# Moving loads, stores and a norm's root within the schedule of a state-space and spectral kernel

## The chip, the cores and the metric

The kernel runs on one core of a Trainium2 chip. The metric is the device time of one execution in microseconds; a kernel's time is the median of several runs. A profile of one execution gives the time of every instruction on the five engines: PE (TensorE, matmuls; PEld is its weight loads), DVE (VectorE), ACT (ScalarE), POOL (GpSimd) and SP (SyncE, which here only issues DMAs).

## The reference

Two layers run one after the other on x of shape (4, 128, 128, 128): batch, channel, height, width. Layer 0 is a selective state-space scan along the 16384 pixels of an image, and a group norm:

```python
h1 = relu(xf @ mlp_w1.T + mlp_b1)
xm = h1 @ mlp_w2.T + mlp_b2
x_in, z = split(xm @ in_proj_w.T, 2)
u = silu(causal_conv4(x_in) + conv_b)
dt, Bm, Cm = split(u @ x_proj_w.T, [8, 24])
delta = softplus(dt @ dt_proj_w.T + dt_proj_b)
A = -exp(A_log)                                  # 256 x 16
def step(h, (d_t, B_t, C_t, u_t)):               # h: batch x 256 x 16
    h = h * exp(d_t[:, :, None] * A) + d_t[:, :, None] * B_t[:, None, :] * u_t[:, :, None]
    return h, einsum('bds,bs->bd', h, C_t)
y = (scan(step) + u * D) * silu(z)
out = y @ out_proj_w.T
x1 = silu(group_norm(out, 4 groups) * gn_w + gn_b) + x
```

Layer 1 filters x1 in the Fourier plane. Weights over four filters come from the image itself:

```python
a = relu(einsum(agg_w, group_norm(concat[x1, x1], 32 groups)) + agg_b)
weights = softmax(mean(a) @ wg_w.T + wg_b)       # batch x 4
xf = rfft2(x1)
ff = rfft2(irfft2(xf[:, None] * wc))             # wc: 4 complex filters a channel
out = irfft2(sum_f weights_f * xf * ff_f) + residual_weight * x1
```

## The kernel before

**Block 0.** An image is cut into 32 chunks of 512 pixels, and the four images make 128 chunks, k = 0 to 127. A chunk takes 16 slots of one hand-written order; slot n of the program belongs to chunk n // 16. In each slot DVE scans a pair of state rows (`scans`, L389, the scan itself in L405), for which ACT has made the decay factors `da` one slot ahead (`exps`, L387) and POOL the inputs `hb` two slots ahead (`dbu`, L354), from copies of delta, du, B and C over the partitions. PE turns one of the inputs by a transpose into PSUM (`b`, L374) and sums the states (`y`, L426).

The chunk's own preparation (`pre`, L175) is a list of steps. Each has a slot, counted from 16 slots before the chunk's scan begins (so its slot 16 is slot 0 of the chunk), a phase and a function. The slots of all chunks go into one table `todo`. In each slot the phases are taken in the order turn, sums, pe, exps, late, act, pool, dbu, gate, scans, dve, end; an engine executes what it gets in this order. DMAs are nearly all issued by SP, also in this order, and SP waits in place when a DMA's buffer or data is not ready. The steps of the preparation that matter here:

- `load` (slot −9): the chunk's input `xt`, 256 KB, one buffer. Chunk 0's is issued by ACT.
- `h1_mm` (−7), `h1_act` (−6), `xm_mm`, `xm_act` (−5, −4): the two layers on PE and ACT; then `cv_mm`, `silu_act` (0 to 2), `xd_mm`, `xd_act` (3, 4). `xd_act` stores `bc` (rows of B and C) to DRAM.
- `bc_load` (5): eight DMAs, which copy B and C to `rB` and `rC` over the partitions (4 x 192 KB and 4 x 256 KB).
- `dt_act` (6): delta, and its two stores to `dd` in DRAM. `du_pool` (7): du = delta * u on POOL, and its two stores.
- `rep_load(0)` (9) and `rep_load(1)` (16): each four DMAs `rdelta` and four `rdu` from `dd`, 256 KB each.

Seen over the repeating 16 slots, the `load` of chunk k at −9 stands in slot 7 of chunk k − 2, beside the `du_pool` of chunk k − 1, and its `h1_mm` in slot 9.

The first slot of all issues the first constants (`first_constants`, L79). Slot 4 issues the later ones (`later_constants`, L105), slot 8 makes products of them on DVE and PE (`later_products`, L123).

**The norm of an image** (`finish`, L552, with `group_norm`, L501, used twice) is spread over the chunks of the next image; for the fourth image it lies in block 1. `group_norm` starts at slot `at`: sums on DVE and a matmul for the mean over groups, ACT's steps one slot later, and in slot `at + 3` all of `var_mm` (PE, into a PSUM bank), `root_act` (ACT, square root, needs another activation table than the exponential) and `invert` (DVE's reciprocal, after which ACT makes scale and bias, or the weights `weff`). `bias_mm` and `bias_act` of the second norm follow in slot `c + 4`, where `c` is its start. `at` is slot 7 of a chunk for the first norm and slot 8 for the second.

**Block 1** has 64 units (8 channels of one image), each in three slots t of 3, 3 and 2 channels: DFT over the height (`over_h`, PE L791, ACT copies `sa` L793, DVE makes the other half L798), over the width (`over_w`), products with the mixed filter on DVE, and back. ACT multiplies four filter tiles by the weights (`term`, L764), POOL adds them (`mix`, L770). Pools open with block 1, so its first loads wait until block 0 has ended: seven constants (L690 to L701), then the unit's input, then the filters. Filter tiles are loaded four units ahead (L741 to L746), the first two both at unit 0. In slot t = 0 the four terms of unit 0 are made ahead of `over_h(0)`.

Of the kernel before, what the change touches and what calls it, by code (L numbers as in the profile page):

```python
# [26 lines left out]
F32 = mybir.dt.float32  # L27
# [7 lines left out]
T = 512  # L35
# [10 lines left out]
def kernel(ctx: ExitStack, tc: tile.TileContext, a: dict, out: bass.AP):  # L46
    nc = tc.nc
# [57 lines left out]
    def later_constants(s):  # L105
        s.wo = const("wo", [P, NH, C], a["out_wT"].rearrange("(j p) c -> p j c", p=P))
        s.gnw = col("gn_w")
        s.gnb = col("gn_b")
        s.g0 = const("g0", [P, P], a["c_g0"])
        s.g1 = const("g1", [P, P], a["c_g1"])  # L110
        s.gam = col("gn_gamma")
        s.bet = col("gn_beta")
        s.wagg = const("wagg", [P, 2, C], a["agg_wT"].rearrange("(j p) o -> p j o", p=P))
        s.bagg = col("agg_b")
        s.wwg = const("wwg", [P, NF], a["wg_wT"])
        s.bwg = const("bwg", [P, NF], a["wg_b"].partition_broadcast(P))
        s.resw = const("resw", [P, 1], a["residual_weight"].partition_broadcast(P))
        s.eps = cpool.tile([P, 1], F32, tag="eps", name="eps")
        nc.vector.memset(s.eps, EPS)
        s.ones = cpool.tile([P, P], F32, tag="ones", name="ones")  # L120
        nc.vector.memset(s.ones, 1.0)
# [25 lines left out]
def block0(tc, s):  # L147
# [4 lines left out]
    with ExitStack() as ctx:  # L152
# [22 lines left out]
        def pre(k):  # L175
# [64 lines left out]
                    )  # L240

            def xd_act():
                xd = d["xd"] = p2.tile([NX, T], F32, tag="xd", name=f"xd_{k}")
                nc.scalar.copy(xd, ps["xd"][0:NX, :])
                bc = d["bc"] = dbc.tile([2, NS, T], F32, tag="bc", name=f"bc_{k}")
                nc.sync.dma_start(out=bc.rearrange("q s t -> (q s) t"), in_=xd[R:NX, :])
# [59 lines left out]
            def rep_load(j):  # L306
# [4 lines left out]
                        nc.sync.dma_start(out=t[m * DG : (m + 1) * DG], in_=rows)  # L311

            return [
                (-9, "pe", load), (-7, "pe", h1_mm), (-6, "act", h1_act), (-5, "pe", xm_mm), (-4, "act", xm_act),
                (0, "pe", partial(cv_mm, 0)), (1, "pe", partial(cv_mm, 1)), (2, "act", silu_act),
                (NP - 3, "pe", z_mm), (NP - 1, "act", z_act), (NP + 2, "act", z_silu), (3, "pe", xd_mm), (4, "act", xd_act), (5, "pe", dt_mm), (5, "pe", xd_turn),
                (5, "act", bc_load), (6, "act", dt_act), (7, "act", xd_turn_act), (7, "pool", partial(du_pool, 0)),
                (7, "pool", partial(du_pool, 1)), (8, "pe", partial(du_turn, 0)), (9, "act", partial(rep_load, 0)),
                (8, "pool", partial(bt_act, 0, 0, 1)), (9, "act", partial(bt_act, 0, 1, 5)),
                (10, "act", partial(bt_act, 0, 5, 8)), (11, "pe", partial(du_turn, 1)),  # L320
# [180 lines left out]
def group_norm(s, io, b, mat, which, stat, at, then):  # L501
# [40 lines left out]
    def invert():  # L542
# [2 lines left out]

    return [
        (at, "dve", aggregate), (at, "end", mean_mm), (at + 1, "act", spread_act), (at + 3, "pe", var_mm),
        (at + 3, "act", root_act), (at + 3, "dve", invert),
    ]


def finish(s, io, b, first, norm, agg, add="dve"):  # L552
# [96 lines left out]
        ]  # L649
    c = at[2] + 5  # L650
    todo += group_norm(s, io, b, "g1", 1, lambda: g["stat"], c, middle)
    todo += [(c + 4, "pe", bias_mm), (c + 4, "act", bias_act)]
    for i in range(NCH):
        at = agg(i)
        todo += [
# [10 lines left out]
def block1(tc, s):  # L666
# [10 lines left out]
    with ExitStack() as ctx:  # L677
        def pool(name, bufs, **kw):
            return ctx.enter_context(tc.tile_pool(name=name, bufs=bufs, **kw))

        p1 = pool("fc", 1)
        p2 = pool("f2", 2)
        psa = pool("psa", 1, space=PSUM)
        psx = pool("psx", 2, space=PSUM)
# [2 lines left out]
        pso = pool("pso", 1, space=PSUM)  # L687
        psf = pool("psf", 1, space=PSUM)

        def const(name, shape):  # L690
            t = p1.tile(shape, F32, tag=name, name=name)
            nc.sync.dma_start(out=t, in_=s.a[name])
            return t

        fh = const("c_fh", [H, 2 * WF])
        fwr = const("c_fwr", [W, 2 * WF])
        fwi = const("c_fwi", [W, 2 * WF])
        ihc = const("c_ihc", [H, H])
        ihs = const("c_ihs", [H, H])
        iw = const("c_iw", [W, W])  # L700
        sign = const("c_sign", [W, 2 * HH]).rearrange("w (o r k) -> w o r k", o=1, r=2)  # L701


        small = pool("small", 1)
# [35 lines left out]
            u[n].ft = ft  # L740
        loads = defaultdict(list)  # L741
        for k, ft in enumerate(spans):
            at = ft.first - 4
            if k >= KEEP:
                at = max(at, spans[k - KEEP].last)
            loads[max(at, 0)].append(ft)  # L746

        def load_filter(ft):
            ft.t = p2.tile([H, NF, CC, 2 * WF], F32, tag="ft", name=f"ft_{ft.first}", bufs=KEEP)
# [9 lines left out]
        def term(n, f):  # L759

            if 0 <= n < N:
                tag, bufs = ("term", 3) if f else ("wb", 2)
                t = p2.tile([H, CC, 2 * WF], F32, tag=tag, name=f"{tag}_{n}_{f}", bufs=bufs)
                nc.scalar.activation(t, u[n].ft.t[:, f], AF.Copy, scale=s.wts[units[n][1]][0:H, f : f + 1])  # L764
                u[n].terms = [t] if f == 0 else u[n].terms + [t]
# [102 lines left out]
        with tc.manual_schedule():  # L868
            load(0)
            for t in range(3 * N + LAG + 3):  # L870
                n, i = divmod(t, 3)
                if i == 0:
                    for ft in loads[n]:
                        load_filter(ft)
                    load(n + 1)
                    if n == 0:
                        for f in range(NF):
                            term(0, f)
                            if f:
# [107 lines left out]
```

## Time and profile before

| | us |
|---|---|
| median of 3 runs (7317.51 to 7325.34) | 7318.06 |
| profiled execution | 7313.21 |
| its span, first to last instruction | 7311.3 |
| block 0 ends, last ACT step before block 1 (L641) | 6495.6 |

| engine | busy us | share of the span | instructions |
|---|---|---|---|
| PE | 5969.1 | 82% | 25908 |
| DVE | 6949.5 | 95% | 8040 |
| ACT | 6148.7 | 84% | 13583 |
| POOL | 6895.5 | 94% | 3188 |

A chunk of block 0 takes about 50 us. The shares are means over two blocks: in block 0 DVE and POOL are nearly full, in block 1 PE is (192.5 of the 200 us from 7000 to 7200). A wait in the profile is the idle time of an engine ahead of an instruction, put down to what came last; a wait of an engine that has time to spare costs nothing. The DMA engines moved 1246.34 MB, 170 GB/s over the span.

### The profile page before, as it was taken

The page shows a single profiled execution, that of the slowest core. Times are in us where ns is not written, and L with a number is a line of the kernel's source. Part 1 is how long each engine was busy: PE and PEld are TensorE (multiplying, and loading weights), DVE is VectorE, ACT ScalarE, POOL GpSimd, SP SyncE. Part 2 cuts the span into 40 slices and gives each one's busy share as a digit, 9 for nine tenths or more (in the row PEclk, how much of TensorE's full clock was granted, in tenths as well). Part 3 has the DMA queues.
Part 4 walks back from the last instruction along what each step waited for, and adds up shares of the span by engine and source line. Part 5 has one row for each costly group of instructions (what it writes and reads, how often), then busy time and mean ns, then how long its engine had stood idle before and what let it go on. Part 6 is the DMA issues. An engine that isn't in the chain of part 4 may idle for free.

```text
span 7311.3 us, 90639 instructions
## 1 busy us (share of the span) xinstructions
PE 5969.1 (82%) x25908; PEld 2667.5 (36%) x25908; DVE 6949.5 (95%) x8040; ACT 6148.7 (84%) x13583; POOL 6895.5 (94%) x3188
## 2 busy tenths in 40 slices
PE   7788877888778788887777888887877888868999
PEld 2233322233223233232222323332322333348999
DVE  7999999999999999999999999999999999978677
ACT  6888888888888888888888888888888888867876
POOL 6999999999999999999999999999999999977787
PEclk8888888888888889989888898888888888889999
DMA  6666666666777767767777766677777766758666
GB/s 140 162 157 146 160 157 150 157 157 163 191 180 180 183 159 168 170 163 180 181 177 192 169 166 169 163 167 179 177 188 177 178 167 157 174 144 250 186 165 170
DMA packets 864136, 1246.34 MB, mean 170 GB/s; under 512 B 78856, under 2 KB 318608, under 8 KB 863632
## 3 DMA queue, kind: packets, MB, share of 16 engines
q1 hardware_dynamic: 863488, 1240.28, 69.0%
q8 instruction: 204, 3.34, 0.2%
q14 instruction: 300, 2.46, 0.1%
q10 hardware_dynamic: 144, 0.26, 0.0%
HBM read 996.97 MB, written 243.27 MB: 170 GB/s over the span
## 4 chain that ended last, share of the span: by engine, by line
DMA 16%; ACT 16%; DVE 12%; PE 12%; issue 5%; POOL 2%; SPq 1%; DVEq 0%; ACTq 0%; POOLq 0%
ACT da L387 6%; DVE da L405 6%; DMA xt<-in_x 3%; DMA rdelta<-dd 3%; DVE h L405 3%; DMA dd<-delta 2%; DVE hb L407 2%; DMA rB<-bc 2%; DMA of<-ob 2%; PE pp_h L190 2%; ACT L387 1%; DMA xr<-in_x 1%; ACT bt L295 1%; PE y L426 1%; PE pa L791 1%
## 5 line engine op out<-in xcount | busy, mean ns | idle before, releaser
L354 POOL TENSOR_TENSOR hb<-rdu,rB 128x1536 f32<-128x1536 f32 (+2 forms) x1536 | 3605.1, 2364 | 33.3 <-DMA rdu<-dd 28.9
L387 ACT ACTIVATE da<-rdelta,amat 128x512 f32<-128x512 f32 x4096 | 2671.9, 694 | 48.2 <-DVE h L405 45.0
L412 POOL TENSOR_TENSOR hb<-h,rC 128x1024 f32<-128x1024 f32 (+1 forms) x1072 | 2434.8, 2273 | 156.0 <-DVE h L405 140.2
L405 DVE TENSOR_TENSOR_SCAN da<-da,st,hb 128x512 f32<-128x512 f32 x1976 | 2420.8, 1268 | 10.0 <-POOL hb L354 6.7
L426 PE MATMUL y<-hb,sel 128*32 128x512 f32 x8192 | 1331.8, 726 | 4.8 <-POOL hb L412 2.9
L405 DVE TENSOR_TENSOR_SCAN h<-da,st,b 128x512 f32<-128x512 f32 x992 | 1261.4, 1272 | 57.8 <-ACT da L387 40.2
L407 DVE TENSOR_TENSOR hb<-da,rC 128x512 f32<-128x512 f32 x2040 | 1297.1, 675 | 3.0
L405 DVE TENSOR_TENSOR_SCAN h<-da,st,hb 128x512 f32<-128x512 f32 x1000 | 1254.1, 1257 | 6.7 <-ACT da L387 6.4
L374 PE MATMUL b<-ident,bt 128*128 128x128 f32 x4096 | 766.1, 311 | 511.8 <-DVE h L405 395.8
L225 PE MATMUL pp_cv<-xm,wck 128*128 128x512 f32 x2048 | 1027.3, 647 | 24.1 <-ACT zs L219 23.2
L295 ACT ACTIVATE bt<-pt_dut,xdt 128x256 f32<-128x256 f32 x2048 | 836.8, 471 | 139.8 <-PE pt_dut L284 139.6
L374 PEld LDWEIGHTS b<-ident,bt 128*128 128x128 f32 x4096 | 557.0, 159 | 1085.7 <-DVE h L405 683.1
L408 ACT COPY st<-da 128x1 f32<-128x1 f32 x2040 | 282.2, 161 | 657.4 <-DVE hb L407 654.6
L225 PEld LDWEIGHTS pp_cv<-xm,wck 128*128 128x128 f32 x2048 | 403.5, 208 | 708.8 <-issue 473.1
L190 PE MATMUL pp_h<-xt,w 128*128 128x512 f32 x512 | 399.5, 925 | 273.0 <-DMA xt<-in_x 257.9
L770 POOL TENSOR_TENSOR wb<-wb,term 128x1040 f32<-128x1040 f32 x192 | 461.0, 2401 | 91.6 <-ACT term L764 76.1
L284 PE MATMUL pt_dut<-ident,du 128*128 128x128 f32 x1024 | 209.6, 328 | 269.6 <-ACT st L408 260.3
L258 PE MATMUL pp_dt<-xd,wdt 8*128 8x512 f32 x512 | 290.1, 649 | 80.1 <-ACT pp_o L450 79.2
L422 PE MATMUL y<-u,diag 128*128 128x512 f32 x512 | 297.2, 665 | 66.6 <-DVE zs L436 65.2
L303 POOL TENSOR_TENSOR du<-delta,u 128x512 f32<-128x512 f32 x256 | 319.3, 1269 | 25.3 <-ACT delta L266 25.3
L387 ACT ACT_TABLE_LOAD x262 | 336.1, 1283 | 4.6
L284 PEld LDWEIGHTS pt_dut<-ident,du 128*128 128x128 f32 x1024 | 128.8, 158 | 565.5 <-POOL du L303 426.8
(145 smaller groups left out, 8008.9 us busy)
## 6 DMA issues: line engine op xcount, KB each, us to landing
rdelta<-dd SPq DMA_DIRECT2D x1024, 256.0 KB, 4.7
rdu<-dd SPq DMA_DIRECT2D x1024, 256.0 KB, 7.7
rC<-bc SPq DMA_DIRECT2D x512, 256.0 KB, 7.4
rB<-bc SPq DMA_DIRECT2D x512, 192.0 KB, 4.7
dd<-delta SPq DMA_DIRECT2D x256, 256.0 KB, 7.5
dd<-du SPq DMA_DIRECT2D x256, 256.0 KB, 6.5
ft<-in_filt_w SPq DMA_DIRECT2D x104, 520.0 KB, 7.0
ob<-o SPq DMA_DIRECT2D x128, 256.0 KB, 2.1
```

Source lines behind the costliest of these rows:

```text
L190: nc.tensor.matmul(ps["h", j], s.w1[:, j * P : (j + 1) * P], d["xt"], start=True, stop=True)
L225: nc.tensor.matmul(ps["cv", j], w, d["xm"][:, t : t + T], start=t == 0, stop=t == KC - 1)
L284: nc.tensor.transpose(ps["dut"][:, 2 * t + j, :], d["du"][:, j, at : at + P], s.ident)
L295: nc.scalar.activation(d["bt"][:, 2 * h + t, :, q, :], src, AF.Copy, scale=d["xdt"][:, 2 * h + t, R + q : R + q + 1])
L354: nc.gpsimd.tensor_tensor(hb[:, p : p + n, :], d["du", j][:, m : m + n, :], d["B"][:, p - 1 : p - 1 + n, :], ALU.mult)
L374: nc.tensor.transpose(b[:, t * P : (t + 1) * P], src, s.ident)
L387: nc.scalar.activation(d["da", p][q], d["delta", j][:, m, :], AF.Exp, scale=s.amat[:, c : c + 1])
L405: nc.vector.tensor_tensor_scan(o, das[q], b, init, ALU.mult, ALU.add)
L407: nc.vector.tensor_tensor(hb[:, p + q, :], das[q], d["C"][:, p + q, :], ALU.mult)
L412: nc.gpsimd.tensor_tensor(hb[:, ps, :], h[:, q, :], d["C"][:, ps, :], ALU.mult)
L426: nc.tensor.matmul(y[m * DG : (m + 1) * DG, :], s.sel, d["hb", j, r][:, p, :], start=False, stop=r == NG - 1)
L770: nc.gpsimd.tensor_tensor(wb, wb, u[n].terms[f], ALU.add)
```

## The change

Five edits, none of which adds or drops an instruction on a computing engine:

1. `load` is placed at slot −14 instead of −9, ahead of the chunk's `bc` store, and `xd` comes from the pool with one buffer instead of two.
2. For chunk 0 alone, `bc_load` is placed at slot 7 instead of 5: behind delta's stores, in phase order still ahead of du's.
3. The seven constants of block 1 are loaded with the later constants of block 0, into the pool that lives through both blocks.
4. In `group_norm`, root and reciprocal are two and three slots later, and with them `bias_mm` and `bias_act` of the second norm, by three and four slots.
5. In block 1 the terms of unit 0 come after `over_h(0)`, and the second filter tile is loaded at unit 1 instead of 0, after the second unit's input.

```diff
@@ later_constants
         s.resw = const("resw", [P, 1], a["residual_weight"].partition_broadcast(P))
+
+        s.fh = const("c_fh", [H, 2 * WF], a["c_fh"])
+        s.fwr = const("c_fwr", [W, 2 * WF], a["c_fwr"])
+        s.fwi = const("c_fwi", [W, 2 * WF], a["c_fwi"])
+        s.ihc = const("c_ihc", [H, H], a["c_ihc"])
+        s.ihs = const("c_ihs", [H, H], a["c_ihs"])
+        s.iw = const("c_iw", [W, W], a["c_iw"])
+        s.sign = const("c_sign", [W, H], a["c_sign"])
@@ xd_act
-                xd = d["xd"] = p2.tile([NX, T], F32, tag="xd", name=f"xd_{k}")
+                xd = d["xd"] = p1.tile([NX, T], F32, tag="xd", name=f"xd_{k}")
@@ pre
-                (-9, "pe", load), (-7, "pe", h1_mm), (-6, "act", h1_act), (-5, "pe", xm_mm), (-4, "act", xm_act),
+                (-14, "pe", load), (-7, "pe", h1_mm), (-6, "act", h1_act), (-5, "pe", xm_mm), (-4, "act", xm_act),
...
-                (5, "act", bc_load), (6, "act", dt_act), (7, "act", xd_turn_act), (7, "pool", partial(du_pool, 0)),
+                (5 if k else 7, "act", bc_load), (6, "act", dt_act), (7, "act", xd_turn_act), (7, "pool", partial(du_pool, 0)),
@@ group_norm
         (at, "dve", aggregate), (at, "end", mean_mm), (at + 1, "act", spread_act), (at + 3, "pe", var_mm),
-        (at + 3, "act", root_act), (at + 3, "dve", invert),
+        (at + 5, "act", root_act), (at + 6, "dve", invert),
@@ finish
-    todo += [(c + 4, "pe", bias_mm), (c + 4, "act", bias_act)]
+    todo += [(c + 7, "pe", bias_mm), (c + 8, "act", bias_act)]
@@ block1
-        fh = const("c_fh", [H, 2 * WF])
...
-        sign = const("c_sign", [W, 2 * HH]).rearrange("w (o r k) -> w o r k", o=1, r=2)
+        fh, fwr, fwi, ihc, ihs, iw = s.fh, s.fwr, s.fwi, s.ihc, s.ihs, s.iw
+        sign = s.sign.rearrange("w (o r k) -> w o r k", o=1, r=2)
...
-            at = ft.first - 4
+            at = max(ft.first - 4, min(k, 1))
             if k >= KEEP:
                 at = max(at, spans[k - KEEP].last)
-            loads[max(at, 0)].append(ft)
+            loads[at].append(ft)
...
-                    if n == 0:
-                        for f in range(NF):
-                            term(0, f)
-                            if f:
-                                mix(0, f)
                 over_h(t)
+                if t == 0:
+                    for f in range(NF):
+                        term(0, f)
+                        if f:
+                            mix(0, f)
```

More of the change, by code (lines that the diff above doesn't have):

```diff
@@ L679, in pool @@
             return ctx.enter_context(tc.tile_pool(name=name, bufs=bufs, **kw))
-        p1 = pool("fc", 1)
         p2 = pool("f2", 2)
@@ L688, in block1 @@
         psf = pool("psf", 1, space=PSUM)
[L690 to L693, printed above, removed]
-        fh = const("c_fh", [H, 2 * WF])
[L696 to L700, printed above, removed]
-        sign = const("c_sign", [W, 2 * HH]).rearrange("w (o r k) -> w o r k", o=1, r=2)
+        fh, fwr, fwi, ihc, ihs, iw = s.fh, s.fwr, s.fwi, s.ihc, s.ihs, s.iw
+        sign = s.sign.rearrange("w (o r k) -> w o r k", o=1, r=2)
         small = pool("small", 1)
```

## The prediction

> **What bounds the kernel now.** I read the page's busy shares first, then the busy time by stretches, then the waits of one engine at a time in the steady part (200 to 6500 us), then the timeline at the four places which the change touches. Four lines give the frame; the stretch's columns are busy us (and instructions) of PE, its weight loads, DVE, ACT and POOL, then granted clock, DMA share and GB/s:
>
> ```profile
> span 7311.3 us, 90639 instructions
> 3000.00:4000.00 1000.00, 796.65 (x3057) 296.11 (x3056) 988.38 (x1044) 864.23 (x1919) 979.42 (x450) 0.88 0.72 176
> DVE h L405 <- ACT da L387: 48.9, 94, 1.4
> DVE rstd L543 <- ACT rstd L540: 13.7, 6, 3.5
> DVE da L405 <- POOL hb L354: 7.9, 8, 1.4
> PE pp_h L190 <- DMA xt<-in_x: 239.2, 116, 5.5
> ```
>
> DVE works 988 of 1000 us, so in block 0 a wait counts only if DVE feels it. PE waits 239 us for the chunk's input, some 2 us a chunk, but that is not the price: DVE waits only some 79 us in these 6300. Of these, some 86 waits of 0.49 us come at one place, after the two ACT table loads around the silu (42 us); the change leaves them. Outside the starts of the images and the norm, some 20 us are left, of 0.2 to 1.4 us each. One of them, from the timeline (start, duration, engine, line; in brackets the idle time and what ended it):
>
> ```profile
> 638.27 3.78 PE L190 MATMUL pp_h<-xt,w 128*128 128x512 f32 x4 [2.11 <-DMA xt<-in_x]
> ...
> 642.09 0.69 ACT L195 ACTIVATE h<-pp_h,mlp_b 128x512 f32<-128x512 f32 x1 [0.97 <-PE pp_h L190]
> ...
> 646.22 0.47 ACT L295 ACTIVATE bt<-pt_dut,xdt 128x256 f32<-128x256 f32 x1 [2.14 <-PE pt_dut L284]
> ...
> 647.57 2.47 DVE L405 TENSOR_TENSOR_SCAN da<-da,st,hb 128x512 f32<-128x512 f32 x2 [0.70 <-ACT da L387]
> ```
>
> The input lands late, PE has idled and runs the four matmuls at 0.95 us each (the form's shortest is 0.59), ACT waits in order, its next `da` is late, DVE stands.
>
> The other three places: a root in block 0, the program's start, and the passage to block 1.
>
> ```profile
> 1734.00 1.28 ACT L540 ACT_TABLE_LOAD   x1
> 1735.30 0.26 ACT L540 ACTIVATE rstd<-pp_gv,eps 128x1 f32<-128x1 f32 x1
> 1735.59 0.17 DVE L543 RECIPROCAL rstd<-rstd 128x1 f32<-128x1 f32 x1 [3.47 <-ACT rstd L540]
> ```
>
> ```profile
> 25.41 1.76 SPq L253 DMA_DIRECT2D rB<-bc  x4
> ...
> 29.16 0.85 SPq L268 DMA_DIRECT2D dd<-delta  x2
> ...
> 49.27 6.83 POOL L354 TENSOR_TENSOR hb<-rdu,rB 128x1536 f32<-128x1536 f32 x2 [21.01 <-DMA rdu<-dd]
> ...
> 78.50 9.07 DVE L126 TENSOR_SCALAR weff<-wagg,gn_gamma 128x128 f32<-128x128 f32 x1
> ```
>
> ```profile
> 6495.66 0.33 SPq L692 DMA_DIRECT2D c_fh<-in_c_fh  x1
> ...
> 6498.93 0.38 SPq L757 DMA_DIRECT2D xt<-x  x1
> ...
> 6503.16 1.64 PE L791 MATMUL pa<-c_fh,xt 128*128 128x130 f32 x6 [9.77 <-DMA xt<-x]
> ...
> 6510.84 1.16 ACT L764 ACTIVATE term<-ft,wts 128x1040 f32<-128x1040 f32 x1 [1.23 <-DMA ft<-in_filt_w]
> 6511.90 0.46 ACT L793 COPY sa<-pa 128x384 f32<-128x384 f32 x1
> 6512.45 0.56 DVE L798 TENSOR_TENSOR sa<-pa,c_sign 128x384 f32<-128x384 f32 x1 [17.15 <-ACT sa L793]
> ```
>
> At the root DVE stands 3.47 us, because reciprocal and root are in one slot. At the start POOL waits for the copies of du. At the passage DVE stands 17 us.
>
> **What the Trainium skill says.** "TensorE: Matmul & The Clock Gate", What's actually happening: after an idle window of about 3.4 us PE gets half its clock. The trace agrees in kind: 0.59 us for the shortest input matmul, 0.95 after a wait. "ScalarE: Activation LUTs", What ACT_TABLE_LOAD costs: 1283 ns and a drain of some 1380 ns. The trace has 1.28 us, and the root starts 0.02 us after it; I use 1.28. "DMA: Bandwidth & Descriptors", Issuing engines are not separate DMA queues: all queues share 16 DMA engines, so a DMA's place counts only where they are full. They are from 27 to 56 us (share 1.05). "SBUF — State Buffer", Who interferes with whom: a tensor_scalar may use the ports shared by DVE and GpSimd, and then waits until GpSimd lets go. That fits L126: 9.07 us, ending as POOL's work at 87.48 ends.
>
> **The change part by part.**
>
> **Input earlier.** SP issues `xt` five slots sooner, after the eight copies of `rep_load(1)` and ahead of the `bc` store. Its buffer was freed by the matmuls nine slots before. SP stood idle there: it waits 1418.8 us in 128 times for `xd`, 11 us a chunk, so 0.4 us of issue and a possible wait for an older DMA of the eight cost nothing. Around the old place, the du stores now pass one 256 KB transfer less (0.65 us at the 400 GB/s that stores ran at), and POOL's 7.9 us of waits for `rdu` in this part should mostly go. PE's wait goes; what is next there is `b` waiting for DVE (384 us), which is harmless. Of DVE's 20 us, I trace four by the same chain as above (before 647, 3710, 5273 and 5983 us). Eight others, 7.9 us, wait for POOL, whose lateness I can only partly put on DMA. I take 12 us; bounds 5 (ACT waits alone, half of them) and 18.
>
> **Roots in block 0.** Six roots, two for each of three images. Removed: 13.7 us, and 1.0 us of `da` waits after the second kind. Added is nothing, but the same two loads and root (1.28 + 0.26 + 1.28 = 2.82 us) now stand ahead of a `da` pair in another slot. In the same stretch of a chunk without a norm (1532 to 1550), that pair starts on ACT at 1541.35 and DVE takes it at 1544.16. With 2.82 us more and a copy, it starts at 4.3 and its first half is done at 4.95: DVE stands 0.85. The three small scale and bias steps (0.9) then delay the next pair, for another 1.5. So 2.35 against a mean of 3.2: 0.9 us an image. The second kind, worked the same way two slots later, gives 1.2 against 1.7. Together some 4.5 us gained in three images. Bounds: 0, and 14.7 if ACT has the slack. The variance bank is held two slots longer; for the second kind the two z matmuls ask for banks in between, a PE wait of under 3 us with `b` waiting behind it, three times, inside these bounds.
>
> **First chunk.** The `xt` of chunk 1 moves to about 8 us, where the DMA engines are idle. Delta's stores go ahead of B and C; du's stay behind. What ends POOL's wait is `rdu`, the last of a full pipe. Bytes in it before: B and C 1.8 MB, `rdelta` and `rdu` 2.1 MB at about 215 GB/s, and 1.3 MB of stores and input at 400: some 21 us from 26.2. After: 0.65 us less, starting some 0.2 later. POOL runs unbroken from 49.27 to 87.48, and L126 ends with it, so all of this shifts: 0.5 us gained (−1 to +1.5, if delta's early stores open or close a gap). PE and ACT get their early work up to 8 us sooner, which POOL hides.
>
> **Constants.** Seven DMAs, 455 KB, move to slot 4 of chunk 0, between the `bc` store and the B and C loads: 7 x 0.47 = 3.3 us of SP. The copies of du for chunk 1 land about 96 now (the DMA engines fall idle at 95.8), so about 99; POOL takes them at 102.5. Nothing; 1 us if that margin of 3.5 is gone.
>
> **Passage.** `xt` goes out at 6495.66 and the filter at 6496.1, each 3.27 us sooner, so the last filter tile has landed at 6507.6 and the terms end at 6508.7. The first DFT, its copy and DVE's statistics are done by then, where before they followed in 6511.90 to 6513.2; so PE's second DFT starts at 6509.85 instead of 6514.2: 4.35 us gained. The second filter is asked for three steps later in the order, but SP runs ahead and it is needed at unit 3. From 6800 PE is 96 to 100% busy, so a shift at the start is kept. Bounds 2 and 6.5.
>
> **Roots in block 1.** DVE waits there 1.23 and 3.86 us; ACT still has the loads, and DVE waits for ACT's `sa` anyway: 1 us of 5, bounds 0 and 5.
>
> `xd` with one buffer: rewritten 16 slots later, its readers are done within 2. Nothing.
>
> Sum: 12 + 4.5 + 0.5 + 4.35 + 1 = 22.4 us. The profiled execution took 7313.2 us (span 7311.3), so 7290.8. The runs shown have a median of 7318.06, 4.8 above it; on that scale 7295.7.
>
> **Rivals.** *Hidden anyway:* DVE's odd waits come from POOL and ACT being nearly full, not from the input. Then input and roots give 2 us, with 5 from start and passage: 7311. For it: DVE is at 98.8%, and most chunks with a 2 us input wait show no DVE wait. Against it: the chain at 647.57. *The clock falls elsewhere (slower):* PE, no longer held by the input, ends its slot early and idles for DVE's scan instead, so that the half-rate stretch meets conv and xd matmuls, which feed silu and `da`, just where DVE already waits 0.49. Its price is the 0.8 us of the two cases at 647 and 5983; in 40 of the 126 chunks, 32 us, less 10 of other gains: 7340. It decides from some 13 chunks on, and would show as a granted clock under the 0.83 to 0.88 of block 0. Against it: PE's idle total doesn't grow. *Roots fit fully* (14.7, not 4.5): 7285; inside my range.
>
> **How the numbers follow.** About 0.2% (14.6 us) is what this measurement can tell. Forecast, with the roots' good end in it: 0.66, a tenth of which ends above 7303.4. Hidden: 0.22, nearly all within 0.2%. Clock: 0.12, nearly all above 7332.7 or close to it. So faster 0.61, within 0.28, slower 0.11. The forecast's own range is 7283 to 7307 (gains of 11 to 35); reaching over the hidden case and its run-to-run spread (7317.5 to 7325.3), 7281 to 7322 leaves out the slow case and the far ends.
>
> **What would show it.** Right: PE's wait for `xt` near nothing; fewer odd DVE waits in 200 to 6500 while the 0.49 ones stay; no DVE wait of its own at L543 but 1 to 2 us for `da` after each root; POOL's first L354 at 48 to 49; the second DFT 4 us nearer to the block's last ACT step. Wrong: odd DVE waits unchanged with PE's wait gone, or waits for `da` at new slots.

## The result, and the profile after

| | before | changed kernel |
|---|---|---|
| median, us | 7319.08 (7317.51 to 7328.17, 6 runs) | 7284.89 (7282.92 to 7287.44, 6 runs) |
| ratio | | 0.9951 [0.9938, 0.9963] |
| profiled execution, us | 7313.21 | 7282.92 |

The kernel got 34.2 us faster in the medians, 0.5%, and 30.3 in the two profiled executions. That of before is one of its quick ones (5.9 us under its median), that of the changed kernel less so (2.0 under), which is the difference of the two gains. Lines of block 0 stand 8 further down in the changed kernel (the scan is L413, `da` L395, `hb` L362, `h1_mm` L198), lines of block 1 three further up.

First the frame: the page's first line, and the same stretch of 1000 us as before (busy us of PE, weight loads, DVE, ACT, POOL, then clock, DMA share, GB/s).

```profile
span 7281.1 us, 90336 instructions
```

```profile
3000.00:4000.00 1000.00, 811.30 (x3065) 298.79 (x3062) 990.79 (x1046) 865.21 (x1924) 982.01 (x451) 0.87 0.75 178
```

DVE still bounds block 0, at 990.79 of 1000 us where it was 988.38. Its waits from 200 to 6500 us in the changed kernel (us in total, times, longest):

```profile
DVE h L413 <- ACT da L395: 42.6, 84, 0.7
...
DVE da L413 <- ACT da L395: 6.8, 11, 0.9
DVE h L413 <- PE b L382: 2.6, 3, 1.0
DVE da L413 <- POOL hb L362: 2.5, 5, 0.5
```

Against before: the first row falls from 48.9 to 42.6 us. The waits of 0.49 us around the silu's table loads stay (77 before, not the prediction's 86, and 70 now); the odd ones above them are gone. The eight put down to POOL are now five short ones, and the reciprocal no longer has a wait of its own; in its place stand six of 0.66 to 0.88 us for `da`. PE's wait for `xt`, 239.2 us before, is not in its list any more; `b` waiting for DVE has grown from 374.9 to 498.7 us in its place (200 to 6460 us).

How fast PE ran after that wait is seen in the input's matmuls (duration in ns: shortest, median, longest, 200 to 6460 us). First before, then the changed kernel:

```profile
L190 PE MATMUL pp_h<-xt,w x492: 592/1061/1224, 240.1 to 6375.0; 128*128 128x512 f32 x164
```

```profile
L198 PE MATMUL pp_h<-xt,w x492: 592/593/1222, 236.7 to 6345.9; 128*128 128x512 f32 x164
```

The median matmul took 1061 ns and takes 593. A chunk has four, which overlap a little: 3.78 us together in the chunk at 638 that the prediction shows, 2.26 in the changed kernel's chunk at 683. So there the input's result reached ACT not 2 us later but 2 + 1.5 = some 3.5. The slow rate didn't begin with the wait for the input: in before the granted clock is 0.50 all the way from 630 to 644 us, after a wait of PE for ACT that ended at 632.28 (3.52 us); in the changed kernel it is 0.53 from 680 to 683 and 0.87 in the two microseconds after, when the input's matmuls run.

Now the three other places of the prediction in the changed kernel's timeline. A root of the first kind:

```profile
1733.72 1.28 ACT L548 ACT_TABLE_LOAD   x1
1735.02 0.26 ACT L548 ACTIVATE rstd<-pp_gv,eps 128x1 f32<-128x1 f32 x1
...
1735.34 1.28 ACT L395 ACT_TABLE_LOAD   x1
1736.63 0.15 DVE L551 RECIPROCAL rstd<-rstd 128x1 f32<-128x1 f32 x1
...
1737.39 1.28 DVE L413 TENSOR_TENSOR_SCAN h<-da,st,b 128x512 f32<-128x512 f32 x1 [0.61 <-ACT da L395]
...
1740.72 2.47 DVE L413 TENSOR_TENSOR_SCAN da<-da,st,hb 128x512 f32<-128x512 f32 x2 [0.88 <-ACT da L395]
```

The reciprocal waits for nothing; DVE pays 0.61 and, behind ACT's three small scale and bias steps, 0.88 us: 1.5 where it paid 3.47. The start:

```profile
47.90 6.82 POOL L362 TENSOR_TENSOR hb<-rdu,rB 128x1536 f32<-128x1536 f32 x2 [21.50 <-DMA rdelta<-dd]
...
77.13 9.09 DVE L134 TENSOR_SCALAR weff<-wagg,gn_gamma 128x128 f32<-128x128 f32 x1
```

POOL starts at 47.90, but the `bc` store was also early here, at 21.86 (before 23.73); from the one to the other it is 26.04 us against 25.54. The passage, whose last ACT step of block 0 ends at 6470.7:

```profile
6471.25 0.37 SPq L754 DMA_DIRECT2D xt<-x  x1
6471.67 5.96 SPq L748 DMA_DIRECT2D ft<-in_filt_w  x4
...
6478.61 0.56 DVE L795 TENSOR_TENSOR sa<-pa,c_sign 128x384 f32<-128x384 f32 x1 [8.25 <-DMA ft<-in_filt_w]
...
6484.62 0.58 PE L534 MATMUL pf_gm<-mv,g 128*128 128x1 f32 x2 [6.68 <-ACT mv L531]
6485.00 1.41 PEld L788 LDWEIGHTS pa<-c_fh,xt 128*128 128x128 f32 x6
6485.07 1.65 PE L788 MATMUL pa<-c_fh,xt 128*128 128x130 f32 x6
```

The first image tile is asked for as soon as block 0 ends, DVE's half of the first DFT no longer stands behind the terms, and the second DFT starts 14.37 us after the block's end instead of 18.57.

To see where the 30.2 us of span come from, both traces were laid side by side by DVE's scans, chunk by chunk:

| part | before | changed | gain |
|---|---|---|---|
| start of program to chunk 1's first scan | 109.51 | 107.92 | 1.6 |
| chunk 1's first scan to chunk 127's | 6331.10 | 6307.75 | 23.4 |
| chunk 127's first scan to the block's last ACT step | 55.02 | 55.02 | 0 |
| from there to the second DFT | 18.57 | 14.37 | 4.2 |
| from there to the end | 797.06 | 796.07 | 1.0 |

Most of the gain is in the repeating chunks, and it is larger there than the 16.5 us (12 + 4.5) that the prediction gave to input and roots. The last row is no more than scatter: the same stretch takes 793.8 to 797.1 us in seven of the eight traces with the old roots (801.0 in e11_ten) and 793.6 to 796.3 in the five with the new.

### The profile page after: what moved, and what is told of

Its sections match the earlier page's. It is cut to its first block, busy times and chain, and to the rows that moved or that the text cites. A ratio compares the mean times of both kernels' runs of the same rounds, so it can differ in the third digit from the quotient of the medians.

```text
span 7281.1 us, 90336 instructions
## 1 busy us (share of the span) xinstructions
PE 5985.5 (82%) x25908; PEld 2647.6 (36%) x25908; DVE 6947.0 (95%) x8040; ACT 6145.5 (84%) x13583; POOL 6894.7 (95%) x3188
## 5 line engine op out<-in xcount | busy, mean ns | idle before, releaser
L362 POOL TENSOR_TENSOR hb<-rdu,rB 128x1536 f32<-128x1536 f32 (+2 forms) x1536 | 3605.3, 2364 | 29.1 <-DMA rdelta<-dd 21.5
L395 ACT ACTIVATE da<-rdelta,amat 128x512 f32<-128x512 f32 x4096 | 2674.0, 695 | 49.2 <-DVE h L413 45.9
L413 DVE TENSOR_TENSOR_SCAN da<-da,st,hb 128x512 f32<-128x512 f32 x1976 | 2419.6, 1267 | 9.5 <-ACT da L395 6.8
L434 PE MATMUL y<-hb,sel 128*32 128x512 f32 x8192 | 1356.1, 739 | 2.9 <-POOL hb L420 2.7
L413 DVE TENSOR_TENSOR_SCAN h<-da,st,b 128x512 f32<-128x512 f32 x992 | 1260.5, 1271 | 60.4 <-ACT da L395 40.3
L413 DVE TENSOR_TENSOR_SCAN h<-da,st,hb 128x512 f32<-128x512 f32 x1000 | 1252.0, 1256 | 0.0
L233 PE MATMUL pp_cv<-xm,wck 128*128 128x512 f32 x2048 | 1050.2, 659 | 32.1 <-ACT zs L227 30.8
L382 PEld LDWEIGHTS b<-ident,bt 128*128 128x128 f32 x4096 | 535.4, 156 | 1195.8 <-DVE h L413 879.7
L430 PE MATMUL y<-u,diag 128*128 128x512 f32 x512 | 315.7, 701 | 171.4 <-DVE zs L444 170.3
L434 PEld LDWEIGHTS y<-hb,sel 128*32 128x32 f32 x8192 | 175.0, 117 | 387.2 <-issue 263.5
```

The lines of the kernel that those rows point to most:

```text
L233: nc.tensor.matmul(ps["cv", j], w, d["xm"][:, t : t + T], start=t == 0, stop=t == KC - 1)
L362: nc.gpsimd.tensor_tensor(hb[:, p : p + n, :], d["du", j][:, m : m + n, :], d["B"][:, p - 1 : p - 1 + n, :], ALU.mult)
L382: nc.tensor.transpose(b[:, t * P : (t + 1) * P], src, s.ident)
L395: nc.scalar.activation(d["da", p][q], d["delta", j][:, m, :], AF.Exp, scale=s.amat[:, c : c + 1])
L413: nc.vector.tensor_tensor_scan(o, das[q], b, init, ALU.mult, ALU.add)
L434: nc.tensor.matmul(y[m * DG : (m + 1) * DG, :], s.sel, d["hb", j, r][:, p, :], start=False, stop=r == NG - 1)
```

## The experiments

The kernels ran four or five times each, e2_root, e3_passage and e4_start thirteen times. The kernel before ran beside all of them, on several chips: 33 runs (7307.94 to 7329.60, median 7318.79) with the first four, nine with each later group (medians 7316.42, 7321.69, 7325.01).

**One edit at a time.** The first theory is the prediction's; its rival is that DVE's odd waits come from POOL and ACT being nearly full.

e1_input: edit 1 alone.

```diff
-                (-9, "pe", load), (-7, "pe", h1_mm), (-6, "act", h1_act), (-5, "pe", xm_mm), (-4, "act", xm_act),
+                (-14, "pe", load), (-7, "pe", h1_mm), (-6, "act", h1_act), (-5, "pe", xm_mm), (-4, "act", xm_act),
-                xd = d["xd"] = p2.tile([NX, T], F32, tag="xd", name=f"xd_{k}")
+                xd = d["xd"] = p1.tile([NX, T], F32, tag="xd", name=f"xd_{k}")
```

> The kernel before with edit 1 alone (input five slots earlier, xd with one buffer). Theory A, the input is the main part: block 0 ends some 18 us earlier than in the kernel before (the trace of after has it 24.9 us earlier, of which 1.6 lie ahead of chunk 1 and about 4 at the roots), so the time falls by 16 to 20 us, PE's wait for xt goes from 239 us in the steady part to under 10, and DVE's odd waits (all but the 0.49 us ones, outside the roots) from some 20 us to under 8. Theory B, the gain needs the edits together or is spread over all of them: under 10 us. Passage and first slots stay as before, apart from the bc, B and C order, which is unchanged here.

Measured 7289.93 us (7287.10 to 7293.27), ratio 0.9959 [0.9947, 0.9972]: 28.9 us by the medians, more than expected. From chunk 1 to chunk 127 it took 6308.3 us, 22.8 less than before. DVE's waits in 200 to 6500:

```profile
DVE h L405 <- ACT da L387: 40.6, 84, 0.7
...
DVE rstd L543 <- ACT rstd L540: 13.2, 6, 3.0
```

All odd waits went, not some: besides those at the silu, the images' starts and the roots, only 1.3 us of the scan's waits is left. DVE's waits in block 0 from 200 us on add up to 58.8 us, before 78.9. So "hidden anyway" is out. One thing in the prediction's account did not happen: POOL's waits for `rdu`, which should mostly have gone, are 9.0 us here and were 7.9.

e2_root: edit 4 alone.

```diff
-        (at + 3, "act", root_act), (at + 3, "dve", invert),
+        (at + 5, "act", root_act), (at + 6, "dve", invert),
-    todo += [(c + 4, "pe", bias_mm), (c + 4, "act", bias_act)]
+    todo += [(c + 7, "pe", bias_mm), (c + 8, "act", bias_act)]
```

> The kernel before with edit 4 alone (root and reciprocal two and three slots later). Theory A, the wait moves from L543 to da two slots on: six waits of 13.7 us go, about 9 come back, and the time falls by 4 to 6 us, of which about 1 in block 1. Theory B, ACT has slack for the table loads: 14 to 18 us. Theory C, what the roots gain is lost again in the chunks after them: 0 to 2 us.

Measured 7312.36 us (7304.69 to 7323.18, 13 runs), ratio 0.9991 [0.9983, 0.9999]: 6.4 us by the medians, 2.6 from chunk 1 to chunk 127 of the two traces. The reciprocal's wait is gone, some 9 us come back as waits for `da` and `b`, as the first theory had it, and PE's wait for `xt` stays (212.8 us).

e3_passage: edits 3 and 5 alone.

```diff
+        s.fh = const("c_fh", [H, 2 * WF], a["c_fh"])
...
+        s.sign = const("c_sign", [W, H], a["c_sign"])
...
-            at = ft.first - 4
+            at = max(ft.first - 4, min(k, 1))
...
-                    if n == 0:
-                        for f in range(NF):
-                            term(0, f)
-                            if f:
-                                mix(0, f)
                 over_h(t)
+                if t == 0:
+                    for f in range(NF):
+                        term(0, f)
+                        if f:
+                            mix(0, f)
```

> The kernel before with edits 3 and 5 alone (block 1's constants in block 0, first DFT ahead of the terms, second filter later). Theory A: block 1's second DFT comes 4.2 us nearer to the last ACT step of block 0 (18.6 us in the kernel before, 13.9 to 14.4 here), block 0 itself is unchanged within 1 us, and the time falls by 4 to 5 us. Theory B, the seven constants in slot 4 of chunk 0 delay the copies of chunk 1: block 0 ends 1 to 3 us later, and the gain is 1 to 3.

Measured 7313.11 us (7305.74 to 7321.05, 13 runs), ratio 0.9992 [0.9984, 1.0001]: 5.7 us by the medians, with an interval that takes in no change. The second DFT starts 13.77 us after the block's last ACT step. Over all traces it starts 17.84 to 18.57 us after it in the seven without edits 3 and 5, and 13.58 to 14.71 in the five with both, so the passage's gain is plain there. Chunk 1 begins no later with the seven constants in its way (107.97 us, before 109.51). Chunk 1 to chunk 127 takes 3.0 us more in this trace than in that of before, chunks lost and won in many places, as kernels with the late input differ among themselves.

e4_start: edit 2 alone.

```diff
-                (5, "act", bc_load), (6, "act", dt_act), (7, "act", xd_turn_act), (7, "pool", partial(du_pool, 0)),
+                (5 if k else 7, "act", bc_load), (6, "act", dt_act), (7, "act", xd_turn_act), (7, "pool", partial(du_pool, 0)),
```

> The kernel before with edit 2 alone (B and C of chunk 0 behind delta's stores). Theory A, all these bytes are ahead of rdu either way, so POOL's first product starts as long after the bc store as before (25.5 us) within 0.7, and the time is unchanged within 2 us. Theory B, the earlier stores let the copies of delta and du start sooner: 2 to 5 us less. The first 20 us can differ between executions by PE's clock, so the distance from the bc store is what counts.

Measured 7319.26 us (7309.03 to 7330.09, 13 runs), ratio 0.9997 [0.9989, 1.0005]: no change. From the `bc` store to POOL's first product it is 26.76 us, before 25.54; the three kernels above, without this edit, have 25.20 to 25.78, two more without it 25.99 (e11_ten) and 26.43 (e10_later), and three more with it 25.46 to 26.51. So a half microsecond here can't be told. The `bc` store itself stands between 21.9 and 26.5 us in the profiled executions, as the matmuls ahead of it run faster or slower (those of `xm_mm` took 0.62 us each in the mean in the changed kernel, 1.05 in before, 1.10 in e2_root).

**Is it PE's wait, or the transfer's place in the queue?** The old load stood ahead of the stores of du. Taking it away there might have been the gain. e5_again keeps the early load and puts a second, unused one where the old one stood:

```diff
+            def again():
+                t = p1.tile([P, T], F32, tag="xa", name=f"xa_{k}")
+                nc.sync.dma_start(out=t, in_=s.xflat[b, :, i * T : (i + 1) * T])
...
-                (-14, "pe", load), (-7, "pe", h1_mm), (-6, "act", h1_act), (-5, "pe", xm_mm), (-4, "act", xm_act),
+                (-14, "pe", load), (-9, "pe", again), (-7, "pe", h1_mm), (-6, "act", h1_act), (-5, "pe", xm_mm), (-4, "act", xm_act),
```

> The early load of e1_input, plus a second, unused load of the same 256 KB into a buffer of its own at the old slot -9. Theory A (PE's wait for the input was what cost): the time stays within 5 us of e1_input's 7289.9, the odd DVE waits stay near 2 us. Rival B (the old transfer stood in the way of the stores of du and of the B and C copies, and the gain is that they run sooner): with the transfer back in its old place the time goes back to 7312 to 7322, and POOL's waits for rdu come back to some 8 us with DVE waits for hb behind them.

Measured 7290.21 us (7285.89 to 7294.70), 0.3 from e1_input. The transfer is back and costs nothing in the medians; DVE's waits put down to POOL are 3.0 us, as against 7.9 before and 1.0 in e1_input. So the transfer's place isn't what cost.

**How much lateness costs how much?** Two doses more of the same edit, on the kernel before: the load one slot later (e10_later, the first added line) and one slot sooner (e11_ten, the second).

```diff
-                (-9, "pe", load), (-7, "pe", h1_mm), (-6, "act", h1_act), (-5, "pe", xm_mm), (-4, "act", xm_act),
+                (-8, "pe", load), (-7, "pe", h1_mm), (-6, "act", h1_act), (-5, "pe", xm_mm), (-4, "act", xm_act),
+                (-10, "pe", load), (-7, "pe", h1_mm), (-6, "act", h1_act), (-5, "pe", xm_mm), (-4, "act", xm_act),
```

> The kernel before with the load one slot later (-8 instead of -9), behind the stores of du instead of ahead of them. Theory A: the input lands some 3 us later in each of 127 chunks, PE's wait for it grows from 239 us to some 550 to 650, and DVE feels it in far more chunks: 7340 to 7420. Rival B (the transfer's place ahead of du's stores costs): du's stores go sooner, so the time falls or stays, 7305 to 7320, whatever PE waits.

Measured 7521.90 us (7510.02 to 7535.10, 4 runs), ratio 1.0281 [1.0267, 1.0295]. The sign is the theory's, the size is far beyond it: 205 us, with PE's wait not even up to the expected 550 (466.1). The waits of DVE in it, and then one instance in the timeline:

```profile
DVE h L405 <- ACT da L387: 196.6, 223, 3.3
DVE rstd L543 <- ACT rstd L540: 21.7, 6, 5.6
DVE da L405 <- POOL hb L354: 15.8, 26, 1.3
```

```profile
1845.01 3.78 PE L190 MATMUL pp_h<-xt,w 128*128 128x512 f32 x4 [3.90 <-DMA xt<-in_x]
...
1848.83 0.69 ACT L195 ACTIVATE h<-pp_h,mlp_b 128x512 f32<-128x512 f32 x1 [0.97 <-PE pp_h L190]
...
1850.16 1.28 DVE L405 TENSOR_TENSOR_SCAN h<-da,st,b 128x512 f32<-128x512 f32 x1 [1.45 <-ACT da L387]
```

It is the chain of the prediction, from the input through slow matmuls (0.95 us each) to ACT and DVE. The first row has 223 waits where before had 94. The wait that PE adds over before is 227 us, the time lost 205, so on this part of the curve a microsecond of PE's wait costs nearly a microsecond.

> The kernel before with the load one slot sooner (-10 instead of -9). A slot is some 3.1 us and PE's mean wait for the input about 2 us. Theory A: one slot is enough, PE's wait for the input falls from 239 us to under 60 and the time to 7288 to 7296, as with -14. Rival (the transfer, now straight behind the B and C copies in a full pipe, lands late all the same, and only a slot ahead of those copies helps): PE's wait stays over 120 us and the time at 7300 to 7318.

Measured 7294.82 us (7292.59 to 7297.34), ratio 0.9967 [0.9954, 0.9979]. Neither account has it whole. PE's wait (the first row below) only halves, which is the rival's number, and yet nearly all of the gain is there. The kernel keeps the two buffers of `xd`, so the one buffer of edit 1 isn't what gains. POOL's waits for `rdu` (the second row) grow to 43.7 us and DVE's waits put down to POOL still fall to 1.7, so these waits of POOL don't reach DVE.

```profile
PE pp_h L190 <- DMA xt<-in_x: 128.7, 83, 4.1
```

```profile
POOL hb L354 <- DMA rdu<-dd: 43.7, 39, 2.4
```

The step between PE and DVE is ACT, which waits ahead of its first step on the input, `h`, only when the matmuls come later than its turn. Its waits there, in before, e11_ten and e10_later (e1_input has none):

```profile
ACT h L195 <- PE pp_h L190: 45.6, 70, 1.0
```

```profile
ACT h L195 <- PE pp_h L190: 6.6, 14, 1.0
```

```profile
ACT h L195 <- POOL hb L354: 134.3, 67, 2.9
ACT h L195 <- PE pp_h L190: 107.2, 119, 1.0
ACT h L195 <- issue: 71.3, 48, 3.5
```

Further rows, of 8.9, 0.3 and 4.3 us, belong to them. Whatever such a row names, `h` starts within 0.1 us of the end of an input matmul in each of these waits, so all of them are waits for the input's matmuls. The four doses together (waits and the input's matmuls from 200 to 6460 us; time as the difference of medians from before in the same group of runs):

| slot of the load | PE's wait for `xt`, us | median input matmul, ns | ACT's wait at `h`, us | time, us |
|---|---|---|---|---|
| −8 (e10_later) | 466.1 | 1061 | 317 | +205 |
| −9 (before) | 239.2 | 1061 | 55 | 0 |
| −10 (e11_ten) | 128.7 | 667 | 7 | −27 |
| −14 (e1_input) | not listed | 593 | none | −29 |

e11_ten is 2 us behind e1_input by this difference, 4.9 by their own medians and 5.9 from chunk 1 to chunk 127, so the first 129 us of PE's wait cost 2 to 6, the next 110 some 17 to 27, the next 227 some 200. ACT's wait has the same bend: PE has a slack of about a microsecond a chunk in the mean, and before stood just past its edge. The wait and the slow matmuls grow together in these doses; no run parts them.

**Were the eight waits waits for POOL?** Eight of DVE's odd waits in before are put down to POOL's `hb`. One of them, in chunk 94 (the lines of POOL and ACT end with the last instruction that was done before the scan began):

```profile
4806.40 3.75 PE L190 MATMUL pp_h<-xt,w 128*128 128x512 f32 x4 [3.78 <-DMA xt<-in_x]
...
4812.13 2.36 POOL L354 TENSOR_TENSOR hb<-rdu,rB 128x1024 f32<-128x1024 f32 x1
...
4814.66 0.69 ACT L387 ACTIVATE da<-rdelta,amat 128x512 f32<-128x512 f32 x1
...
4815.44 2.47 DVE L405 TENSOR_TENSOR_SCAN da<-da,st,hb 128x512 f32<-128x512 f32 x2 [1.20 <-POOL hb L354]
```

POOL's product was done at 4814.49, 0.95 us before the scan started; ACT's `da` was done at 4815.35, 0.09 before. In all eight the scan starts 0.09 us after the end of a `da`, and 0.19 to 0.96 us after POOL's last product. So these were waits for ACT too, and in seven of them ACT had waited for `pp_h` a few microseconds earlier: the same chain.

**The parts within the changed kernel.** With the load at −8 or −9 a kernel's runs lie 11 to 25 us apart (4 to 33 runs each), with it sooner 4 to 9 (5 or 6 runs each), so single edits are better taken away from the changed kernel. e9_noroot is the changed kernel without edit 4:

> The changed kernel with edit 4 undone (root, reciprocal and the bias steps in their old slots). If the roots' move is worth what the prediction gave it (4.5 us in block 0 and 1 in block 1), 7288 to 7292 against 7284.9, with a DVE wait of some 13 us in 6 instances at the reciprocal. Rival: with the input early ACT catches up by itself, or the small waits of eight chunks that the changed kernel shows come with the root's new slots: 7283 to 7286, no loss.

Measured 7288.26 us (7285.39 to 7290.83): 3.4 us by the medians. The steps of the two traces at the roots alone add up to 5.0 us over three images, and chunk 1 to chunk 127 takes 3.9 us longer. Besides the roots, single chunks differ by 0.6 us either way between the two traces, five such steps one way, eight the other. Against e1_input, which has the old roots too, the steps at the roots add up to 4.4 us, but chunk 1 to chunk 127 is only 0.5 us shorter in the changed kernel: the same eight chunks (62, 88, 90, 93, 94, 120, 122 and 125) take 0.5 to 0.6 us more there. The four traces with early load and new roots have seven to nine such chunks, the three with early load and old roots none, five and five. So part of what the roots gain is lost again in later chunks, as the third theory of e2_root had it. At the roots the prediction's 4.5 us hold; over block 0 it is 0.5 to 3.9. By which step it is lost stays open.

e12_no5 is the changed kernel without edit 5:

```diff
-            at = max(ft.first - 4, min(k, 1))
+            at = ft.first - 4
...
+                    if n == 0:
+                        for f in range(NF):
+                            term(0, f)
+                            if f:
+                                mix(0, f)
                 over_h(t)
-                if t == 0:
-                    for f in range(NF):
-                        term(0, f)
-                        if f:
-                            mix(0, f)
```

> The changed kernel with edit 5 undone: the constants are there early, but both first filters are asked for at unit 0 and the terms of unit 0 stand ahead of the first DFT again. If the early constants carry most of the passage (3.27 of the predicted 4.35 us), the second DFT starts some 15.3 us after block 0's last ACT step (changed kernel 14.4, before 18.6) and the time is 1 us up, 7285 to 7287. Rival (the order of terms and DFT carries it, since ACT and DVE still follow the last filter tile): 17 to 18.5 us and 7288 to 7289.

Measured 7287.06 us (7283.52 to 7289.57), 2.2 up by medians whose ranges overlap. The second DFT starts 14.93 us after the block's end: of the 4.2 us of the passage the early constants carry 3.6 and the order of terms and DFT 0.6, the second hardly more than the 13.58 to 14.71 us of the traces with both can tell. In its timeline the old order is seen (its block 0 ends at 6477.0):

```profile
6488.56 1.16 ACT L761 ACTIVATE term<-ft,wts 128x1040 f32<-128x1040 f32 x1 [0.65 <-DMA ft<-in_filt_w]
6489.62 0.46 ACT L790 COPY sa<-pa 128x384 f32<-128x384 f32 x1
6490.17 0.56 DVE L795 TENSOR_TENSOR sa<-pa,c_sign 128x384 f32<-128x384 f32 x1 [13.51 <-DMA ft<-in_filt_w]
6490.29 3.60 SPq L754 DMA_DIRECT2D xt<-x  x2
6491.47 0.50 PEld L534 LDWEIGHTS pf_gm<-mv,g 128*128 128x128 f32 x2 [8.51 <-ACT mv L531]
```

DVE idles 13.51 us instead of 8.25, since the copy `sa` follows the terms. But what releases PE's next matmul is the statistics, and they come only half a microsecond later than in the changed kernel.

**A better start.** The prediction held that POOL's first product waits for bytes in a full pipe. C isn't needed for it. e7_c_later is the changed kernel with chunk 0's four copies of C behind the first copies of delta and du:

```diff
-                (5 if k else 7, "act", bc_load), (6, "act", dt_act), (7, "act", xd_turn_act), (7, "pool", partial(du_pool, 0)),
+                *([(5, "act", bc_load)] if k else
+                  [(7, "act", partial(bc_load, "B")), (10, "act", partial(bc_load, "C"))]),
+                (6, "act", dt_act), (7, "act", xd_turn_act), (7, "pool", partial(du_pool, 0)),
```

> The changed kernel with chunk 0's four copies of C (1.05 MB) behind the copies of delta and du. If POOL's first product waits for bytes in a full pipe, 1.05 MB at some 215 GB/s less stands ahead of rdu: the stretch from the bc store to the first product falls from some 26 us to 21, and the time by 3 to 5 us, to 7280 to 7282. Rival (something else ends last at the start, or C is then late for the first sums): the stretch or DVE's start doesn't move and the time stays at 7284 to 7287.

Measured 7279.86 us (7278.33 to 7282.20), ratio to before 0.9950 [0.9938, 0.9963]. The ratio can't tell it from the changed kernel (0.9951), because before scatters; by its own runs it can: all five are under the changed kernel's lowest, by 5.0 us in the medians. Against e9_noroot, which ran in turns with it on one chip, it is 8.4 us faster, which leaves 3.4 to 5.0 for C when 3.4 to 5.0 are taken off for the roots. In the trace the `bc` store is at 24.94:

```profile
45.30 6.82 POOL L364 TENSOR_TENSOR hb<-rdu,rB 128x1536 f32<-128x1536 f32 x2 [15.83 <-DMA rdu<-dd]
```

From the store to the first product it is 20.36 us instead of 26.04, and from the store to chunk 1's first scan 81.07 instead of 86.06, so most of these 5.7 us are in the time. They fit the account of bytes, which expected some 5 (1.05 MB at 215 GB/s is 4.9 us), though four fewer issues of SP also stand ahead, which no run parts from the bytes. Edit 2 moved other bytes, and those gained nothing.

The other thing at the start was L134 (L126 before), which holds DVE for 9 us. e8_both is e7_c_later with this product on ACT:

```diff
-        nc.vector.tensor_scalar_mul(weff0, s.wagg[:, 0, :], s.gam[:, 0:1])
+        nc.scalar.activation(weff0, s.wagg[:, 0, :], AF.Copy, scale=s.gam[:, 0:1])
```

> e7_c_later with the first product of the later constants (chunk 0, the 9.07 us multiplication by a scalar) on ACT instead of DVE. If that instruction, which waits for GpSimd to let go, holds back DVE's first scans, up to 9 us and at least 3 go: 7271 to 7277. Rival (as in e3_passage, where it took 3.20 us and chunk 1 began no sooner): POOL sets the start of the scans, and the time stays within 2 us of e7_c_later's 7279.9.

Measured 7280.13 us (7278.55 to 7284.12), the same as e7_c_later. In its trace of DVE the hold has only moved on:

```profile
75.22 7.59 DVE L135 SCALAR_TENSOR_TENSOR weff<-wagg,gn_gamma,weff 128x128 f32<-128x128 f32 x1 [1.48 <-ACT weff L134]
82.73 0.15 DVE L140 TENSOR_TENSOR bias<-pp_bias,agg_b 128x1 f32<-128x1 f32 x1
```

The second product, 0.35 us in e7_c_later, now takes 7.59, until POOL's unbroken work ends (82.66 us). So a start without any such hold wasn't tried. Two other traces show what it could be worth: in e3_passage and e11_ten the first product took 3.20 and 3.23 us and the second 2.34 and 2.33, and chunk 1's first scan came 58.7 and 56.2 us after POOL's first product, in the eleven others 59.9 to 60.7. So the remark in the last expectation, that chunk 1 began no sooner in e3_passage, doesn't stand: by this distance it began over a microsecond sooner.

## Why the prediction was right, and where it was off

The forecast was 7296 us, a gain of 22.4; the gain was 34.2, with the sign expected and within the range, near its fast end (the forecast's own range ended at gains of 11 and 35). Two terms were off by much, in opposite directions: in the traces the input gave 22.8 us instead of 12, the roots in block 0 added 0.5 instead of 4.5. So it is in part luck that the sum is no further off. By its steps:

- *Input earlier, 12 us (5 to 18).* This term was mis-sized, and it is most of the miss. By itself it gave 28.9 us in the medians and 22.8 in the chunks of the profiled executions; no run takes it away from the changed kernel. The mechanism was right (e5_again, the doses, and the chain in e10_later). The step that failed is "Of DVE's 20 us, I trace four by the same chain ... Eight others, 7.9 us, wait for POOL, whose lateness I can only partly put on DMA. I take 12 us". The eight were waits for ACT's `da` under another name, seven of them at the end of the very chain that the term is about, and nearly all of the 20 went: with 20 in place of 12 the sum is 30.4, and the traces gained 30.2. The upper bound of 18 was under the 20 us that the same paragraph had counted. Also, PE's own price was read as its idle time, though the prediction quotes matmuls of 0.95 us after it: the four slow matmuls add 1.5 us to the 2 by which ACT's input is late.
- *The profiled execution as the base.* It was 5.9 us quicker than before's median, and the gain on it was carried over unchanged to the medians. 3.9 us of the miss are this. The spread of before's runs, 11 to 23 us, goes with the late input (4 to 9 us without it), so a quick execution is presumably one in which this very cost was low; that wasn't looked at in a trace of a slower one.
- *Roots in block 0, 4.5 us.* Right at the roots and too high for the block. The steps there are 4.4 us against e1_input and 5.0 against e9_noroot, but from chunk 1 to chunk 127 only 0.5 and 3.9 are left, as later chunks take longer. The term's own figures, 0.9 and 0.5 us an image, make 4.2, not 4.5. The worked waits for the first kind were 0.85 and 1.5, together 2.35; the trace has 0.61 and 0.88. The three z waits of PE for a bank, put inside the bounds, did appear: 2.6 us of DVE's time in all.
- *First chunk, 0.5 us (−1 to +1.5).* Nothing that can be measured (e4_start). The 1.6 us that the changed kernel's trace shows come from its early `bc` store (21.86, before 23.73). That POOL started at 47.90, as forecast, is for the same reason luck.
- *Constants, 0.* Right: from the `bc` store to chunk 1's first scan it is 86.06 us in the changed kernel, before 85.78; the shorter way in e3_passage (84.08) goes with the shorter hold of DVE there.
- *Passage, 4.35 us.* Measured 4.2, and 3.1 to 5.0 over all pairs of traces without and with edits 3 and 5. That the earlier loads (3.3) carry most of it is confirmed by e12_no5 (3.6).
- *Roots in block 1, 1 us.* Not shown: the stretch after the second DFT is 1.0 us shorter here, but 1.3 shorter still in e9_noroot, with the old roots.
- *The rivals.* "Hidden anyway" falls with e1_input. "The clock falls elsewhere" falls too: the granted clock in the stretch is 0.87 against 0.88, from 200 to 6460 us it is 0.87 against 0.86, and no DVE waits came at conv's place. In e10_later its opposite is seen: late input, slower time. "Roots fit fully" named 7285, the number that came, but the six waits of 0.66 to 0.88 us for `da` and e9_noroot show that the roots don't fit fully.

What stays open: what makes the seven to nine later chunks longer when the roots are moved, and how much of the input's price is PE's wait and how much the slow matmuls that go with it.

## What to carry to other kernels

A wait of an engine that has time to spare costs nothing only within its slack, and its total of waits doesn't show the slack: here about a microsecond a chunk was nearly free, the next one cost a quarter at most, and beyond that nearly all of it counted. So find where on this curve a kernel stands by moving the load one step each way, and look at whether the engine behind it has begun to wait (here ACT at `h`: 7, 55 and 317 us). Where an engine ahead of the bounding one waits for its input in nearly every round, price the bounding engine's odd waits together, not only those that could be traced. And before a wait is put down to the engine that a profile names, compare the end of that engine's work with the start of the wait's instruction: here the named one had been done for up to 0.96 us, and another ended 0.09 us before. Where the DMA engines are full, ask which bytes the first consumer needs, and move the others behind.

## What the runs showed that was not expected

- A late input makes a kernel's time uncertain: those with a PE wait of 200 us and more had runs 11 to 25 us apart, those with 129 us or none 4 to 9.
- The Trainium skill ("SBUF — State Buffer", Who interferes with whom) has DVE and GpSimd lock each other out of a shared port pair. Here an instruction of DVE that fits this was held through several operations of GpSimd in a row: 9.07 us (L126), until POOL's unbroken work ended. In e3_passage it ended as one of POOL's operations did and took 3.20 us. In e8_both the hold passed to the next such instruction (7.59 us for one that took 0.35).
- Taking PE's slow rate away in the input matmuls (1061 to 593 ns) hardly moved the mean granted clock (0.88 and 0.87 from 3000 to 4000 us, 0.86 and 0.87 from 200 to 6460): PE idles elsewhere instead, ahead of `b`, and DVE's waits for `b` are 2.6 us in all.
